# Attention with four heads at once, one in each quarter of the partitions, by tiles of queries

## The chip, the cores and the metric

The kernel runs on one core of a Trainium2 chip. The metric is device time in microseconds (us), from the first to the last work of one execution. All arithmetic is float32.

## The reference, cut to what matters

Two layers follow each other; each adds an attention branch and a feed-forward branch to its input `x` of 4 batches x 512 tokens x 512 features. The change lies in the attention of the second layer (`L1_attn`):

```python
c_kv = hidden_states @ W_DKV + b_DKV                 # 128 latent features
k = (c_kv @ W_UK + b_UK).reshape(b, s, H, D)         # H = 16 heads, D = 128
v = (c_kv @ W_UV + b_UV).reshape(b, s, H, D)
c_q = hidden_states @ W_DQ + b_DQ                    # 384 latent features
q = (c_q @ W_UQ + b_UQ).reshape(b, s, H, D)
q_r = q @ W_QR                                       # 128 -> 64
k_r = k @ W_KR
def rope(x):
    x1, x2 = (x[..., :half], x[..., half:])          # half = 32
    first = x1 * cos - x2 * sin
    return jnp.concatenate([first, jnp.zeros_like(first)], axis=-1)
q = q.at[..., :RD].set(rope(q_r))                    # RD = 64
k = k.at[..., :RD].set(rope(k_r))
scores = jnp.einsum('bqhd,bkhd->bhqk', q, k) / jnp.sqrt(jnp.float32(D))
probs = jax.nn.softmax(scores, axis=-1)
ctx = jnp.einsum('bhqk,bkhd->bqhd', probs, v).reshape(b, s, H * D)
return ctx @ W_O + b_O
```

Of the 128 features of a head, 64 are plain, 32 are rotated and 32 are zero, so a score is a sum over 96 products: three times 32.

## The kernel before, in words

The program has three stretches. From 0 to about 970 us come the first layer (a test-time-training attention and a ternary feed-forward, whose products all go through the helper at L117) and the latents of the second. From there to 1138.5 us runs the second layer's mixture of experts (pools `d_...`, products at L969, L1032 and L1062), with the preparation of the attention's first weights beside it (`fold`, biases, cosines and sines, and `lv`, the key latents with tokens on partitions). The rest, to the end at 2031.2 us, is the attention (pools `e_...`).

**Weights.** The 16 heads are four groups `hg` of four (`HPG`). `fold` prepares a group: it multiplies the rotated part into the up-projection weights (`uk`, `uq0` to `uq2`, products `pw`, L868) and W_UV into W_O (`vo`, products `pvo`, L886), so that values are never formed: a context is a product of probabilities with the key latents `lv`, and the output a product of contexts with `vo`. `fold` is a generator; one step of it is taken in a head's turn, ahead of the group that needs it.

**One head.** The attention loops over 64 units (group, batch, head).
- `queries_keys` makes kT and qT, 96 features x 512 tokens: one product for pk (L1174), three for pq (L1182). ScalarE (ACT) copies the 64 plain rows with their bias (L1175, L1186). `rotate` makes the 32 rotated rows: two operations on VectorE (DVE; L1157, L1163, each bias and cosine or sine) and a subtraction on GpSimd (POOL, L1167).
- `exponentials` makes the scores of one tile of 128 queries x 512 keys (sc, L1192), the negated row maximum on DVE (mx, L1194) and the exponential on ACT with its row sum (L1197). `scaled` is the reciprocal on DVE (L1201) and the scaling on ACT (L1202).
- `softmax` transposes each tile of probabilities in blocks of 32x32 on DVE (tt, L1221). `turn` brings the blocks to their partitions with 16 DMAs from SyncE's queue (SP; prT, L1252), each 64 KB: 32 partitions with four runs of 512 bytes.
- `context` is four products over the keys (pc, L1260) and a copy on ACT into ctxT (L1262).
- When the four heads of a (group, batch) have contexts, `outputs` multiplies ctxT with vo in four steps, by Strassen's seven products of halves with one bank `px` that is read between partial sums (p and px, L1303; 256-column products). The sums of its left operands run on POOL, and DVE adds the results into y (L1324). The last (group, batch) goes through `project_out` instead (po, L1360), with whole products.
- The first and the last head turn their probabilities by transposes on TensorE (`turned_at_once`).

**Order.** `pin` keeps the order on an engine as the program gives it. In the turn of unit i stand, one after the other: the projections of head i, scores and softmax and the turn of head i-1, one step of the outputs of a finished (group, batch), the context of head i-3, a step of `fold`. prT has three buffers; scores have four PSUM banks (ps_sc), projections, contexts, outputs and folds share three (ps_pj), and px has one.

Of the kernel before, what the change touches and what calls it, by code (L numbers as in the profile page):

```python
# [18 lines left out]
P = 128  # L19
# [36 lines left out]
def trunk_kernel(ctx: ExitStack, tc: tile.TileContext, a: dict, out: bass.AP):  # L56
# [761 lines left out]
    trig_k = lat.tile([P, L], F32, tag="trig_k", name="trig_k")  # L818
    trig_q = lat.tile([P, L], F32, tag="trig_q", name="trig_q")
    wqr = lat.tile([P, RD], F32, tag="W_QR", name="W_QR")  # L820
    wkr = lat.tile([P, RD], F32, tag="W_KR", name="W_KR")
    buk = lat.tile([P, H], F32, tag="b_UK", name="b_UK")
    buq = lat.tile([P, H], F32, tag="b_UQ", name="b_UQ")
# [11 lines left out]
    bo_part = lat.tile([P, HS], F32, tag="bo_part", name="bo_part")  # L835
    ones = lat.tile([P, P], F32, tag="ones", name="ones")
# [8 lines left out]
    def group_tiles(pool, hg):  # L845
        w = {nm: pool.tile([P, HPG, D], F32, tag=nm, name=f"{nm}_{hg}", bufs=1) for nm in ups}
        w["vo"] = pool.tile([P, HPG, HS], F32, tag="vo", name=f"vo_{hg}", bufs=1)
        return w

    def fold(w, hg, wk, psum, bufs, ahead=1, rows=nc.sync):  # L850

        heads = slice(hg * HPG, (hg + 1) * HPG)
        for nm, src in zip(ups, up_srcs):
            nc.sync.dma_start(out=w[nm][:, :, :RD], in_=src.rearrange("p (h d) -> p h d", h=H)[:, heads, :RD])
# [7 lines left out]
        for i in range(n + 1 + ahead):  # L862
            k = i - ahead - 1
            if 0 <= k < n - 1:
                wt, wr, to = turned.pop(k), wqr if k else wkr, w[ups[k]]
                pw = psum(f"pw_{hg}_{i}").rearrange("p (h d) -> p h d", h=HPG)[:, :, :RD]
                for h in range(HPG):
                    pin(nc.tensor.matmul(pw[:, h, :], lhsT=wt[:, h, :], rhs=wr, start=True, stop=True))  # L868
                pin(nc.scalar.copy(to[:, :, RD:], pw))
# [13 lines left out]
        wt = turned.pop(n - 1)  # L883
        for h in range(HPG):
# [17 lines left out]
    with ExitStack() as px:  # L902
# [197 lines left out]
        for e in range(E):  # L1100
            if e == 1:
# [7 lines left out]
                first = fold(w0, 0, wk, lambda nm: psp.tile([P, 512], F32, tag="pa", name=nm), 1)  # L1109
                nc.sync.dma_start(out=buk, in_=a["b_UK"])  # L1110
                nc.sync.dma_start(out=buq, in_=a["b_UQ"])
                for k in range(E):
                    nc.sync.dma_start(
                        out=trig_k[RD:, :].rearrange("p (k e j) -> p k e j", k=NCHUNK, e=E)[:, :, k],
                        in_=a["trig"][:, k * P : (k + 1) * P].rearrange("p (k j) -> p k j", k=NCHUNK),
                    )
# [6 lines left out]
            if e == 2:  # L1123

                for wr, bias in ((wkr, buk), (wqr, buq)):
                    pb = psp.tile([P, 512], F32, tag="pa", name="pb")
                    nc.tensor.matmul(pb[RD:, :H], lhsT=wr, rhs=bias, start=True, stop=True)
                    nc.vector.tensor_copy(bias[RD:, :], pb[RD:, :H])
                pb = psp.tile([P, 512], F32, tag="pa", name="pbuv")
                nc.tensor.transpose(pb[:, :H], buv16, ident[:H, :H])  # L1130
                nc.vector.tensor_copy(buv, pb[:, :H])
                nc.vector.tensor_scalar_mul(buq[:RD, :], buq[:RD, :], scale)
                tc.keep_in_program_order(nc.vector.tensor_scalar_mul(trig_q[RD:, :], trig_k[RD:, :], scale))
# [12 lines left out]
    with ExitStack() as px:  # L1146
# [5 lines left out]
        def rotate(t, ps, bias, trig, nm):  # L1152

            mid = RD + HALF
            t1 = wk.tile([P, L], F32, tag="t1", name=f"t1_{nm}")
            pin(
                nc.vector.scalar_tensor_tensor(  # L1157
                    t1[RD:mid, :], ps[RD:mid, :], bias[RD:mid, :], trig[RD:mid, :], ALU.add, ALU.mult
                )
            )  # L1160
            t2 = wk.tile([P, L], F32, tag="t2", name=f"t2_{nm}")
            pin(
                nc.vector.scalar_tensor_tensor(  # L1163
                    t2[RD:mid, :], ps[mid:, :], bias[mid:, :], trig[mid:, :], ALU.add, ALU.mult
                )
            )
            nc.gpsimd.tensor_sub(t[RD:mid, :], t1[RD:mid, :], t2[RD:mid, :])  # L1167

        def queries_keys(hg, b, h, w):
            nm = f"{hg}_{b}_{h}"  # L1170
            hh = hg * HPG + h
            kT = wk.tile([P, L], F32, tag="kT", name=f"kT_{nm}")
            pk = ps_pj.tile([P, L], F32, tag="pj", name=f"pk_{nm}")
            pin(nc.tensor.matmul(pk, lhsT=w["uk"][:, h, :], rhs=ckv[:, b, :], start=True, stop=True))  # L1174
            pin(nc.scalar.activation(kT[:RD, :], pk[:RD, :], AF.Identity, bias=buk[:RD, hh : hh + 1], scale=1.0))  # L1175
            rotate(kT, pk, buk[:, hh : hh + 1], trig_k, f"k{nm}")
            qT = wk.tile([P, L], F32, tag="qT", name=f"qT_{nm}")
            pq = ps_pj.tile([P, L], F32, tag="pj", name=f"pq_{nm}")
            nq = QC // P
            for i in range(nq):  # L1180
                pin(
                    nc.tensor.matmul(  # L1182
                        pq, lhsT=w[f"uq{i}"][:, h, :], rhs=cqs[hg, b][:, i, :], start=(i == 0), stop=(i == nq - 1)
                    )
                )
            pin(nc.scalar.activation(qT[:RD, :], pq[:RD, :], AF.Identity, bias=buq[:RD, hh : hh + 1], scale=scale))  # L1186
            rotate(qT, pq, buq[:, hh : hh + 1], trig_q, f"q{nm}")
            return qT, kT

        def exponentials(qT, kT, i, nm):  # L1190
            ps = ps_sc.tile([P, L], F32, tag="sc", name=f"sc_{nm}_{i}")
            pin(nc.tensor.matmul(ps, lhsT=qT[:KQ, i * P : (i + 1) * P], rhs=kT[:KQ, :], start=True, stop=True))  # L1192
            mx = wk.tile([P, 1], F32, tag="mx", name=f"mx_{nm}_{i}", bufs=4)
            pin(nc.vector.tensor_reduce(mx, ps, AX.X, ALU.max, negate=True))  # L1194
            sm = wk.tile([P, 1], F32, tag="sm", name=f"sm_{nm}_{i}", bufs=4)
            pr = wk.tile([P, L], F32, tag="pr", name=f"prob_{nm}_{i}", bufs=4)
            pin(nc.scalar.activation(pr, ps, AF.Exp, bias=mx, scale=1.0, accum_out=sm))  # L1197
            return pr, sm

        def scaled(pr, sm):  # L1200
            pin(nc.vector.reciprocal(sm, sm))  # L1201
            pin(nc.scalar.mul(pr, pr, sm))  # L1202
            return pr

        def probabilities(qT, kT, nm):

            last = None
            for i in range(E):
                now = exponentials(qT, kT, i, nm)
                if last:  # L1210
                    yield scaled(*last)
                last = now
            yield scaled(*last)

        def softmax(qT, kT, nm):

            tt = wk.tile([P, L // 32, 2, E, K], F32, tag="tt", name=f"tt_{nm}")

            def turn_blocks(i, pr):
                pin(  # L1220
                    nc.vector.transpose(  # L1221
# [310 lines left out]
```

## Time and profile before

| | |
|---|---|
| median of 3 runs | 2030.62 us (2025.25 to 2031.38) |
| the profiled execution: time and span | 2031.2 us, in one span that starts with the first and ends with the last work |
| busy share of the span | TensorE (PE) 97%, DVE 65%, ACT 42%, POOL 31% |
| attention stage, first pk at 1138.5 us to the end | 892.7 us; PE busy 882.3, DVE 646.3, ACT 478.7, POOL 277.9 |
| largest groups in that stage | scores 230.6 us busy in 512 passes, contexts 219.6 in 488 recorded, pq 175.3 in 384, pk 66.0 in 128 |

The profile counts each float32 product as two passes of the systolic array; "x8" is four products. "Busy" of a pass is from its start to its modelled end, and passes overlap, so the distance from start to start is the price of a pass. A line names the engine, the line of the kernel, the operation, "output<-inputs", the shape as partitions x elements, and how many. In the timeline a row is a run of like instructions, with its start and its length in us. A DMA is issued by an engine's queue (SPq is SyncE's): its row there is the time of the issue, and "to landing" the time from the start of the issue until the data are there.

### The profile page before, as it was taken

How to read it: one execution, taken by the hardware profiler on the slowest of the kernel's cores; microseconds unless marked ns; L12 is line 12 of the kernel's file. 1: busy time of each engine (PE TensorE's matmuls, PEld its weight loads, DVE VectorE, ACT ScalarE, POOL GpSimd, SP SyncE). 2: the span in 40 equal slices, each digit the busy share in tenths (PEclk: the TensorE clock that was granted, in tenths of full speed). 3: DMA queues.
4: the chain of work that ended last, by engine and by line, in shares of the span. 5: the costliest groups of instructions: out<-in, count | busy, mean ns of one | idle time of the engine just before them, and what ended most of it. 6: DMA issues, size and time to landing. Idle time of an engine off the chain costs nothing.

```text
span 2031.2 us, 30926 instructions
## 1 busy us (share of the span) xinstructions
PE 1970.7 (97%) x10550; PEld 1258.7 (62%) x10550; DVE 1318.6 (65%) x2760; ACT 863.1 (42%) x1763; POOL 631.4 (31%) x707
## 2 busy tenths in 40 slices
PE   8999999999999999998999999999999999999999
PEld 6777676767767676744777645555555555555555
DVE  5545657475666565664555787777777777777773
ACT  2233334334334342421322365555555555555552
POOL 4334342434243342421000232223223232354320
PEclk9999999999999999999999999999999999999999
DMA  6757566646465465645821144344434443433333
GB/s 161 208 132 210 142 181 168 182 120 180 115 168 166 127 182 150 210 136 186 290 82 57 57 106 116 94 106 112 109 94 113 106 112 81 101 98 89 93 98 94
DMA packets 318472, 270.92 MB, mean 133 GB/s; under 512 B 87659, under 2 KB 239404, under 8 KB 317676
## 3 DMA queue, kind: packets, MB, share of 16 engines
q1 hardware_dynamic: 298080, 237.31, 43.2%
q0 software_dynamic: 8736, 26.31, 4.4%
q10 hardware_dynamic: 11500, 5.32, 0.9%
q8 instruction: 85, 1.39, 0.3%
q14 instruction: 71, 0.58, 0.1%
HBM read 174.18 MB, written 34.87 MB: 103 GB/s over the span
## 4 chain that ended last, share of the span: by engine, by line
PE 48%; DVE 2%; ACT 1%; SPq 0%; issue 0%; DMA 0%; DVEq 0%; ACTq 0%
PE pc L1260 10%; PE sc L1192 10%; PE pq L1182 8%; PE px L1303 5%; PE p L1303 4%; PE epg L969 3%; PE pk L1174 3%; PE epu L969 1%; PE epo L1032 1%; PE po L1360 1%; PE eox L1062 1%; PE pw L868 1%; PE pvo L886 1%; ACT prob L1197 1%; PE eo L1062 1%; SPq L1252 0%
## 5 line engine op out<-in xcount | busy, mean ns | idle before, releaser
L1197 ACT ACTIVATE prob<-sc,mx 128x512 f32<-128x512 f32 x256 | 174.3, 683 | 164.2 <-DVE mx L1194 159.4
L1192 PE MATMUL sc<-kT,qT 96*128 96x512 f32 x512 | 230.6, 592 | 1.5 <-DVE prT_head L1241 1.3
L1260 PE MATMUL pc<-prT,lv 128*128 128x512 f32 x488 | 219.6, 592 | 0.4 <-DMA prT<-tt 0.4
L1221 DVE STREAM_TRANSPOSE tt<-prob 128x512 f32<-128x512 f32 x248 | 170.3, 706 | 55.1 <-ACT prob L1202 45.7
L1167 POOL TENSOR_TENSOR kT<-t_k,t_k 32x512 f32<-32x512 f32 x64 | 80.6, 1259 | 380.3 <-PE pq L1182 235.6
L117 PE MATMUL pf<-xT,wg 128*128 128x256 f32 x704 | 174.1, 389 | 5.7 <-DMA wg<-in_wg 3.6
L1182 PE MATMUL pq<-cq,uq 128*128 128x512 f32 x384 | 175.3, 592 | 1.7 <-ACT ctxT L1262 1.7
L1202 ACT ACTIVATE prob<-prob,sm 128x512 f32<-128x512 f32 x256 | 176.5, 713 | 0.0
L1192 PEld LDWEIGHTS sc<-kT,qT 96*128 96x128 f32 x512 | 96.8, 190 | 124.1 <-issue 118.2
L117 PE MATMUL pf<-xT,wu 128*128 128x256 f32 x704 | 169.6, 384 | 3.3 <-DMA wu<-in_wu 3.3
L1194 DVE TENSOR_REDUCE mx<-sc 128x1 f32<-128x512 f32 x256 | 168.0, 677 | 2.3 <-PE sc L1192 0.3
L117 PE MATMUL pd<-wd,hid 128*128 128x512 f32 x352 | 165.7, 600 | 0.9 <-DMA wd<-in_wd 0.7
L117 PEld LDWEIGHTS pf<-xT,wg 128*128 128x128 f32 x704 | 132.7, 193 | 32.4 <-issue 9.3
L1260 PEld LDWEIGHTS pc<-prT,lv 128*128 128x128 f32 x488 | 92.5, 190 | 92.9 <-issue 88.8
L117 PEld LDWEIGHTS pf<-xT,wu 128*128 128x128 f32 x704 | 135.1, 193 | 23.4 <-DMA wu<-in_wu 4.7
L478 DVE SCALAR_TENSOR_TENSOR hid<-pf,us,sg 128x256 f32<-128x256 f32 x88 | 41.8, 477 | 159.5 <-ACT sg L477 159.1
L1182 PEld LDWEIGHTS pq<-cq,uq 128*128 128x128 f32 x384 | 72.8, 190 | 93.9 <-issue 81.8
L314 POOL TENSOR_SCALAR sk<-k,m 128x256 f32<-128x256 f32 x64 | 60.6, 957 | 180.1 <-PE pz L117 167.9
L421 POOL TENSOR_SCALAR gh<-grad,m 128x256 f32<-128x256 f32 x64 | 61.6, 972 | 152.0 <-DVE grad L390 130.2
L117 PEld LDWEIGHTS pd<-wd,hid 128*128 128x128 f32 x352 | 63.5, 190 | 59.4 <-issue 44.0
L477 ACT ACTIVATE sg<-pf,gs 128x256 f32<-128x256 f32 x88 | 41.4, 473 | 135.9 <-PE pf L117 135.5
L1167 POOL TENSOR_TENSOR qT<-t_q,t_q 32x512 f32<-32x512 f32 x64 | 80.6, 1260 | 56.3 <-DVE t_q L1163 56.3
(326 smaller groups left out, 3579.0 us busy)
## 6 DMA issues: line engine op xcount, KB each, us to landing
prT<-tt SPq DMA_DIRECT2D x992, 64.0 KB, 2.0
wd<-in_wd SPq DMA_DIRECT2D x176, 256.0 KB, 3.1
wg<-in_wg SPq DMA_DIRECT2D x88, 256.0 KB, 3.0
wu<-in_wu SPq DMA_DIRECT2D x88, 256.0 KB, 3.2
cq<-lat_d SPq DMA_DIRECT2D x48, 256.0 KB, 3.9
rows<-rows SPq DMA_DIRECT2D x128, 66.0 KB, 2.2
kv<-rows POOLq DMA_DIRECT2D x32, 264.0 KB, 4.3
gu<-in_gu SPq DMA_DIRECT2D x3, 2048.0 KB, 8.6
```

What stands on the lines that cost most here:

```text
L117: nc.tensor.matmul(out, lhsT=lhsT, rhs=rhs, start=start, stop=stop, skip_group_check=True)
L421: nc.gpsimd.tensor_scalar_mul(gh[:, :, h, :], g, m2[:, h : h + 1])
L969: nc.tensor.matmul(ps, lhsT=w[:, c, :], rhs=x[:, c], start=start and c == 0, stop=c == 1, skip_group_check=True)
L1167: nc.gpsimd.tensor_sub(t[RD:mid, :], t1[RD:mid, :], t2[RD:mid, :])
L1182: nc.tensor.matmul(pq, lhsT=w[f"uq{i}"][:, h, :], rhs=cqs[hg, b][:, i, :], start=(i == 0), stop=(i == nq - 1))
L1192: pin(nc.tensor.matmul(ps, lhsT=qT[:KQ, i * P : (i + 1) * P], rhs=kT[:KQ, :], start=True, stop=True))
L1194: pin(nc.vector.tensor_reduce(mx, ps, AX.X, ALU.max, negate=True))
L1197: pin(nc.scalar.activation(pr, ps, AF.Exp, bias=mx, scale=1.0, accum_out=sm))
L1202: pin(nc.scalar.mul(pr, pr, sm))
L1221: nc.vector.transpose(out=tt[:, :, :, i, :], in_=pr.rearrange("p (kb e j) -> p kb e j", e=2, j=K))
L1260: pin(nc.tensor.matmul(pc, lhsT=lv[:, b, k, :], rhs=prT[:, k, :], start=(k == 0), stop=(k == E - 1)))
L1303: nc.tensor.matmul(ps[:, q, :], lhsT=a[:, k, q * P : (q + 1) * P], rhs=w[:, k, :], start=start and k == 0 and q == 0, stop=k == 1, skip_gr ...
```

## The change

The unit becomes one (group, batch) with four heads at once, and a block of work one tile of 128 queries for these four heads. The three pieces of 32 features (even plain, odd plain, rotated) lie in tiles of their own; in each, head h has the partitions 32h to 32h+31. There are again 64 blocks: 16 units of four query tiles.

- `fold` writes the weights in two halves, plain and rotated (cosine part of all four heads, sine part of all four), with the score's scale multiplied in; the tile for vo is allocated later.
- `up_projected` makes 128 columns (32 of each of four heads) for keys and for queries: one and three products again. Pieces 0 and 1 are a bias copy on ACT over 128 partitions. Pieces 2 and 3 are one DVE operation each over 128 partitions, and the subtraction on POOL runs over 128 partitions. One of the four is made in each block, for the next unit, in the order 2, 3, 0, 1.
- `scores` issues 12 products of 32 rows for a block, round the four row quarters, each head into a bank of its own.
- `softmax` interleaves the four heads' steps; `prT` has two buffers, and each of the 16 DMAs now moves one 2 KB run from each of 32 partitions.
- The context of block n-1 stands behind the scores, the projections, the output step and the fold step of block n.
- The outputs of the last unit take the same Strassen steps, with one more bank and the left sums on DVE; finished quarters are stored as they come. The transposes on TensorE for the first and last head and `project_out` are gone.
- In the mixture stage, cosine and sine are copied to all four quarters by six more DMAs on SP, and the biases come from 32 small products, each into a quarter of the columns.

The diff, without the removed functions, which are shown above:

```diff
-    trig_k = lat.tile([P, L], F32, tag="trig_k", name="trig_k")
-    trig_q = lat.tile([P, L], F32, tag="trig_q", name="trig_q")
+    cos, sin = (lat.tile([P, L], F32, tag=nm, name=nm) for nm in ("cos", "sin"))
-    buk = lat.tile([P, H], F32, tag="b_UK", name="b_UK")
-    buq = lat.tile([P, H], F32, tag="b_UQ", name="b_UQ")
+    b_up = lat.tile([P, 2, E, NHG], F32, tag="b_up", name="b_up")
...
     def group_tiles(pool, hg):
+        return {nm: pool.tile([P, 2, HPG * RD], F32, tag=nm, name=f"{nm}_{hg}", bufs=1) for nm in ups}
...
-                pin(nc.scalar.copy(to[:, :, RD:], pw))
+                pin(
+                    nc.scalar.mul(
+                        to[:, 1].rearrange("p (x h r) -> p h x r", x=2, h=HPG),
+                        pw.rearrange("p h (x r) -> p h x r", x=2),
+                        scale if k else 1.0,
+                    )
+                )
...
+                for t, rows in ((cos, slice(0, HALF)), (sin, slice(HALF, RD))):
+                    for k in range(E):
+                        nc.sync.dma_start(
+                            out=t[:HALF].rearrange("p (k e j) -> p k e j", k=NCHUNK, e=E)[:, :, k],
+                            in_=a["trig"][rows, k * P : (k + 1) * P].rearrange("p (k j) -> p k j", k=NCHUNK),
+                        )
+                    for r in quarters[1:]:
+                        nc.sync.dma_start(out=t[r], in_=t[:HALF])
                 nc.sync.dma_start(out=ckv, in_=lat_d[0].rearrange("p b k x -> p b (k x)"))
...
+                for j, wr in enumerate((wkr, wqr)):
+                    by_head = b_raw[:, j].rearrange("p (hg h) -> p h hg", h=HPG)
+                    for m in range(E):
+                        t = ident[:, m:RD:2] if m < 2 else wr[:, HALF * (m - 2) : HALF * (m - 1)]
+                        for h, r in enumerate(quarters):
+                            nc.tensor.matmul(
+                                pb[r, j, m],
...
+        def up_projected(u, m, to):
+            hg, b = u
+            def columns(w):
+                return w[:, 0, m::2] if m < 2 else w[:, 1, (m - 2) * P : (m - 1) * P]
+            nq = QC // P
+            for j, nm in enumerate("kq"):
+                ps = ps_pj.tile([P, L], F32, tag="pj", name=f"p{nm}_{hg}_{b}_{m}")
+                srcs = [(f"uq{i}", cqs[u][:, i, :]) for i in range(nq)] if j else [("uk", ckv[:, b, :])]
+                for i, (w, x) in enumerate(srcs):
+                    pin(
+                        nc.tensor.matmul(
+                            ps, lhsT=columns(ws[hg][w]), rhs=x, start=(i == 0), stop=(i == len(srcs) - 1)
+                        )
+                    )
+                bias = b_up[:, j, m, hg : hg + 1]
+                if m == 2:
+                    t1 = to[f"t1{nm}"] = wk.tile([P, L], F32, tag="t1", name=f"t1{nm}_{hg}_{b}")
+                    pin(nc.vector.scalar_tensor_tensor(t1, ps, bias, cos, ALU.add, ALU.mult))
+                elif m == 3:
+                    t = to[f"{nm}2"] = wk.tile([P, L], F32, tag=f"{nm}r", name=f"{nm}r_{hg}_{b}")
+                    pin(nc.vector.scalar_tensor_tensor(t, ps, bias, sin, ALU.add, ALU.mult))
+                    nc.gpsimd.tensor_sub(t, to.pop(f"t1{nm}"), t)
+                else:
+                    t = to[f"{nm}{m}"] = wk.tile([P, L], F32, tag=f"{nm}{m}", name=f"{nm}{m}_{hg}_{b}", bufs=2 - m)
+                    pin(nc.scalar.activation(t, ps, AF.Identity, bias=bias, scale=scale if j else 1.0))
+                yield
+        def scores(qk, i, nm):
+            ps = [ps_sc.tile([P, L], F32, tag="sc", name=f"sc_{nm}_{i}_{h}") for h in range(HPG)]
+            for n, c in enumerate((0, 2, 1)):
+                for h, r in enumerate(quarters):
+                    pin(
+                        nc.tensor.matmul(
+                            ps[h],
+                            lhsT=qk[f"q{c}"][r, i * P : (i + 1) * P],
+                            rhs=qk[f"k{c}"][r, :],
+                            start=(n == 0),
+                            stop=(n == 2),
+                        )
+                    )
+            return ps
+        def softmax(ps, nm, to):
+            tt = wk.tile([P, 4, HPG, E, 32], F32, tag="tt", name=f"tt_{nm}")
+            prs = {}
+            for h in range(HPG + 2):
+                if h < HPG:
+                    mx = wk.tile([P, 1], F32, tag="mx", name=f"mx_{nm}_{h}", bufs=4)
+                    pin(nc.vector.tensor_reduce(mx, ps[h], AX.X, ALU.max, negate=True))
+                    sm = wk.tile([P, 1], F32, tag="sm", name=f"sm_{nm}_{h}", bufs=4)
+                    pr = wk.tile([P, L], F32, tag="pr", name=f"prob_{nm}_{h}", bufs=4)
+                    pin(nc.scalar.activation(pr, ps[h], AF.Exp, bias=mx, scale=1.0, accum_out=sm))
+                    prs[h] = pr, sm
+                if 0 <= h - 1 < HPG:
+                    pr, sm = prs[h - 1]
+                    pin(nc.vector.reciprocal(sm, sm))
+                    pin(nc.scalar.mul(pr, pr, sm))
+                if h >= 2:
+                    pr, sm = prs.pop(h - 2)
+                    pin(
+                        nc.vector.transpose(
+                            out=tt[:, :, h - 2], in_=pr.rearrange("p (k kq j) -> p kq k j", kq=4, j=32)
+                        )
+                    )
+                if h < HPG + 1:
+                    yield
+            prT = to[nm] = wk.tile([P, 4, HPG, E, 32], F32, tag="prT", name=f"prT_{nm}")
+            for qb in range(4):
+                for kq in range(4):
+                    nc.sync.dma_start(out=prT[32 * kq : 32 * kq + 32, qb], in_=tt[32 * qb : 32 * qb + 32, kq])
+            yield
+        def context(prT, b, ctxT, i, nm):
+            pc = ps_pj.tile([P, L], F32, tag="pj", name=f"pc_{nm}")
+            at = prT.rearrange("p qb h k j -> p (qb h) k j")
+            for k in range(E):
+                pin(nc.tensor.matmul(pc, lhsT=lv[:, b, k, :], rhs=at[:, :, k, :], start=(k == 0), stop=(k == E - 1)))
+            pin(
+                nc.scalar.copy(
+                    ctxT.rearrange("p eh h el (i c j) -> p i c (eh h el) j", c=2, j=K)[:, i],
+                    pc.rearrange("p (c x j) -> p c x j", c=2, j=K),
+                )
+            )
...
-        def left_operands(c):
+        def left_operands(c, eng):
...
+            final = (hg, b) == (NHG - 1, B - 1)
...
+            def store(qh, oh):
+                if hg == NHG - 1:
+                    for e in (2 * qh, 2 * qh + 1):
+                        cols = slice(oh * half, (oh + 1) * half)
+                        nc.sync.dma_start(out=rows_of(out, b)[:, e, cols], in_=y[b][:, e, cols])
...
+            o = left_operands(c, nc.vector if final else nc.gpsimd)
...
+            if final:
+                p4 = bank(ps_sc, "sc", "p4")
+                block_product(p4, o["a22"], r["t4"])
+                add(p4, 1, 0)
             block_product(x, o["s2"], r["t2"], False)
             add(p2, 0, 0)
+            store(0, 0)
             add(x, 0, 1)
...
+        units = [(hg, b) for hg in range(NHG) for b in range(B)]
+        nu = len(units)
+        order = (2, 3, 0, 1)
+        ws, cs, qk, probs = {0: w0}, {}, {}, {}
+        folds, outs = iter(()), iter(())
+        def advance(n, steps):
+            for _ in range(n):
+                next(steps, None)
+        def context_of(n):
+            u, i = divmod(n, E)
+            hg, b = units[u]
+            if i == 0:
+                cs[u] = wk.tile([P, 2, HPG, 2, P], F32, tag="ctxT", name=f"ctxT_{u}")
+            context(probs.pop(f"{u}_{i}"), b, cs[u], i, f"{u}_{i}")
+        cqs[units[1]] = batch_latents(*units[1])
+        qk[0] = {}
+        for m in order:
+            for _ in up_projected(units[0], m, qk[0]):
+                pass
+        for u, (hg, b) in enumerate(units):
+            if b == 0 and hg + 1 < NHG:
+                pool = (lat, wk)[(hg + 1) % 2]
+                ws[hg + 1] = group_tiles(pool, hg + 1)
+                folds = fold(
+                    ws[hg + 1],
+                    pool,
+                    hg + 1,
+                    wk,
+                    lambda nm: ps_pj.tile([P, 512], F32, tag="pj", name=nm),
+                    2,
+                    2,
+                    nc.gpsimd,
+                )
+            if u + 2 < nu:
+                cqs[units[u + 2]] = batch_latents(*units[u + 2])
+            qk[u + 1] = {}
+            for i in range(E):
+                n = E * u + i
+                soft = softmax(scores(qk[u], i, f"{u}"), f"{u}_{i}", probs)
+                ups_next = up_projected(units[u + 1], order[i], qk[u + 1]) if u + 1 < nu else iter(())
+                advance(2, soft)
+                advance(1, ups_next)
+                advance(1, soft)
+                advance(1, ups_next)
+                advance(1, soft)
+                if u > 0 and i == 1:
+                    outs = outputs(*units[u - 1], ws[units[u - 1][0]], cs.pop(u - 1))
+                advance(1, outs)
+                advance(1, soft)
+                advance(1, folds)
+                if n > 0:
+                    context_of(n - 1)
+                advance(1, soft)
+                if hg == NHG - 1:
+                    nc.gpsimd.tensor_add(y[b][:, i, :], y[b][:, i, :], bo)
+            qk.pop(u)
+        advance(1, outs)
+        context_of(E * nu - 1)
+        for _ in outputs(*units[-1], ws[NHG - 1], cs.pop(nu - 1)):
+            pass
```

## The prediction

> **What bounds the kernel now.** I read the page first: span, engines, and the chain that ended last.
>
> ```profile
> span 2031.2 us, 30926 instructions
> ...
> PE 1970.7 (97%) x10550; PEld 1258.7 (62%) x10550; DVE 1318.6 (65%) x2760; ACT 863.1 (42%) x1763; POOL 631.4 (31%) x707
> ...
> PE pc L1260 10%; PE sc L1192 10%; PE pq L1182 8%; PE px L1303 5%; PE p L1303 4%; PE epg L969 3%; PE pk L1174 3%; PE epu L969 1%; PE epo L1032 1%; PE po L1360 1%; PE eox L1062 1%; PE pw L868 1%; PE pvo L886 1%; ACT prob L1197 1%; PE eo L1062 1%; SPq L1252 0%
> ```
>
> The chain is TensorE. The attention stage runs from the first pk at 1138.5 to the end, 892.7 us, and the windows put TensorE busy there in 98% or more, DVE near 74%, ACT near 55%. So TensorE work that goes is gained as long as nothing else becomes late. The timeline gives the prices:
>
> ```profile
> 1986.61 1.89 PE L1303 MATMUL p<-vo,ctxT 128*128 128x256 f32 x8
> ...
> 1987.88 10.25 SPq L1252 DMA_DIRECT2D prT<-tt  x16
> ...
> 1988.34 1.89 PE L1303 MATMUL px<-t_ops,s_ops 128*128 128x256 f32 x8
> ...
> 1990.06 3.60 PE L1192 MATMUL sc<-kT,qT 96*128 96x512 f32 x8
> ...
> 1993.50 1.89 PE L1303 MATMUL p<-t_ops,s_ops 128*128 128x256 f32 x8
> ```
>
> A float32 product is two passes. From the start of one row to the start of the next, a 512-column pass takes 3.44/8 = 0.43 us and a 256-column pass 1.73/8 = 0.216 us, whether 96 or 128 rows are used. Beside it stands the row this prediction turns on: SP needs 10.25 us to issue the 16 DMAs that turn one head's probabilities, 0.64 us each. A head takes 892.7/64 = 13.9 us, and a head's probabilities have two heads' time before they are read, so today that costs nothing.
>
> For small products side by side the trace has the column-tiled ones of the first stage:
>
> ```profile
> 415.84 0.59 PE L117 MATMUL pz<-gsum,bones 128*128 128x256 f32 x2
> 416.37 1.08 PE L117 MATMUL pz<-wq_bd,sk 128*32 128x128 f32 x32
> 417.27 0.63 PE L117 MATMUL pso<-wq_bd,wh 128*32 128x64 f32 x32
> 417.83 1.09 PE L144 MATMUL pj<-ident,xt 128*128 128x128 f32 x8
> 418.76 0.59 PE L117 MATMUL pd<-wd,hid 128*128 128x512 f32 x1
> ```
>
> 32 passes of 128 columns start within 0.90 us, 28 ns each; the full-width transposes of the same length take 0.93/8 = 116 ns. Four column tiles run at once, in float32, issued round the four tiles as the new scores will be. Going in and out costs: two 256-column passes want 0.43 us and take 0.53, so 0.1; out about the same, 0.1 to 0.2.
>
> **The change, part by part.** A block is one tile of 128 queries for four heads; 64 blocks replace 64 heads.
>
> Scores. Before: 512 passes x 0.43 = 220 us. After: per block 12 products, 24 passes, four at a time, so 6 x 0.43 = 2.58, plus two switches of 0.15 = 2.88; x 64 = 184. Gain 36. Row tiles are not in the trace; bounds: four at once (column row, 2.58) to none at once (24 x 0.43 = 10.3). I take the column row: same machine, same float32, same issuing order.
>
> The rule that speaks against it is in the Trainium skill, "TensorE: Matmul & The Clock Gate", Part 3, "Measured speedup vs the span model": four row tiles gave 3.07 times there, not 4. By the page a set would take 0.56 us, 50 us more TensorE work. The column row says 116/28, about 4, and I sum by it.
>
> A dearer set has a row of its own: pso, the same column tiles with 64 columns. Its 32 passes take 0.56 us (417.27 to 417.83), 17.5 ns each, where half of a 128-column pass at the 256-column rate is 0.216/4 = 0.054: 3.1 times. I hold this for the short pass (the new ones have 512 columns), and keep it as the upper bound: sets of 0.43 x 4/3.1 = 0.56, so 64 x 6 x 0.13 = 50 us more.
>
> Projections and contexts keep their counts, 512 passes each: 220 + 220. Outputs: before 15 units x 56 x 0.216, 32 passes of 0.43 and 32 transposes of 0.11 = 199; after 16 x 56 x 0.216 = 194. Folds 23 in both. Without waits the stage is 184 + 220 + 220 + 194 + 23 = 841, plus about 7 of head and tail (the first block waits on its rotation, the last context copy, the last add and store: 3.9 us lie behind the last matmul now) = 848, against 892.7: 45 us less.
>
> Off the path: the 256 rotations of 32x512 on DVE (0.75 us each) become 64 of 128x512, 128 subtractions on POOL (1.26) become 32, 128 bias copies on ACT become 64. DVE and ACT are not the bound, so I cost this at nothing.
>
> Earlier stages: 32 tiny column-tiled products for the biases (32 passes of 128x4 take 0.8 us in the trace), 1.5 us on TensorE. The cosine and sine copies hold SP some 9 us instead of 3 and are ahead of ckv, wanted only 25 us later: nothing.
>
> The probabilities' turn is where a wait is added. Before, the context of head i-3 stands after the scores of head i-1: two heads' slack, three prT buffers. After, the context of block n-1 stands on TensorE behind the scores, projections and output step of block n: one block's slack. Behind a waiting context on TensorE queue the next scores, so a late turn stops everything. Follow it from the end of block n-1's scores. The order of the built program puts the output step's adds on DVE ahead of the last two transposes. So: switch 0.15, projections 3.44, output step 3.46, result 0.2 = 7.25; add 0.69, reciprocal 0.16, scale on ACT 0.71, last transpose 0.71 = 9.5. Then 16 issues on SP, and the last lands 1.43 us after its issue ends (median of the 992 prT DMAs now: 2.0 from start, 0.6 of it issue). Each new DMA moves one 2 KB run from each of 32 partitions instead of four of 512 B. Its issue is not in the trace. The nearest rows, back to back:
>
> ```profile
> 775.84 1.29 SPq L625 DMA_DIRECT2D xl<-xe_d  x3
> ...
> 30.63 5.61 SPq L294 DMA_DIRECT2D rows<-rows  x12
> ...
> 227.57 1.88 SPq L127 DMA_DIRECT2D xt<-in_x  x3
> ...
> prT<-tt SPq DMA_DIRECT2D x992, 64.0 KB, 2.0
> ```
>
> xl (128 partitions, one 2 KB run each) 0.43; rows (16 partitions) 0.47; xt (64 partitions, one 2 KB run each) 0.63; prT (32 partitions, four runs) 0.64. Number of runs and bytes don't order these: 128 runs cost 0.43 and 0.64. The count of partitions does: 128 and 16 cheap, 64 and 32 dear. Bounds 0.43 to 0.64; I take 0.64, because the new DMA has the partitions of the one and the single run of the other dear row.
>
> So the turn is there 9.5 + 10.3 + 1.43 = 21.2 us after the scores. Context 3.44, then the next scores 0.15 + 2.58: 27.4 us for two blocks, 54.8 for a unit of four. TensorE's own work is 2.88 + 3.44 + 3.46 + 3.44 = 13.2 a block, 11.5 where a unit's output begins, 51.2 a unit. Wait: 3.6 x 14 middle units = 51. The first unit has no outputs (last transpose at 8.2): 26.2 against 19.6 for two blocks, 12 us. The last has no projections (7.9): 12 us, and 6 for the last block's turn. Folds put 23 us of products into the waiting, but also a transpose of 0.7 on DVE ahead of the chain: I take 5 off. 51 + 12 + 12 + 6 - 5 = 76.
>
> Sum: -45 + 76 + 1.5 = +32 on the profiled 2031.2. That execution lies 0.6 above the median 2030.6, so 2062.
>
> The Trainium skill would leave the wait out: "DMA: Bandwidth & Descriptors", "Issuing engines are not separate DMA queues", calls the time to initiate a DMA usually small beside the DMA. Here it is 0.64 beside 2.0, and 16 stand in a row. By the page the stage would be 848 and the kernel 1987; the row decides.
>
> **Rivals.** *The issue gets cheap, faster.* If one run per partition costs 0.47 (rows), the turn is there at 9.5 + 7.5 + 1.43 = 18.4, and two blocks need 24.6, under the 25.6 of TensorE's work: no wait in the middle units. First unit 8, last 7, end 4.5: 20 in all. -45 + 20 + 1.5 = -24: 2007. For it: fewer descriptors, as few as rows' or fewer. Against: xt has one run per partition and costs 0.63. It decides at about 0.575 us an issue, where waits are worth 45.
>
> *Row products run two at a time, much slower.* Sets of 0.86: 165 us more TensorE work, waits shrink to about 26: -45 + 165 + 26 + 1.5, 2180. All one after another, near 2490. For it: the two passes of one product share a row tile, and four banks are written at once, which no row shows. Against: the column tiles have the same two passes.
>
> *Between*: an issue of 0.55 to 0.6, or a chain about 1 us shorter than I add up: 2025 to 2037.
>
> **How the numbers follow.** Forecast case (0.64, four at once) 0.58, its own range 2040 to 2092: down 22 if the chain is 0.75 us shorter than I add up (two chains in a unit, so 1.5 x 15 units); up 30 for sets of 0.56 by the pso row, 50 us of work of which some 20 only fill waits. Cheap issue 0.22 (2000 to 2024). Between 0.09. Rows in twos or worse 0.11. A range of 2003 to 2092 leaves out the last case and the ends of the first two. About 0.3%, 6 us, is what a measurement of this kernel can tell from no change. Faster 0.24 (cheap issue and a little), same 0.09, slower 0.67.
>
> **What would show it.** Right: prT issues at 0.64 us on SP; TensorE idle put down to DMA prT in front of the contexts, 60 to 80 us in all, most in the first and last unit per block; score sets of four starting within tens of ns, 0.43 us a set; DVE's share falling. Wrong: issues near 0.45 and no such idle time; score passes at over 0.11 us each on average; TensorE waiting for DVE or ACT instead.

## The result, and the profile after

The changed kernel takes 2091.28 us (median of 4 runs, 2087.96 to 2101.61), beside 2028.95 us for the kernel before in the same rounds: ratio 1.031, 95% interval 1.028 to 1.035. The forecast was 2062, a loss of 31 us; the measured loss of 62 us is twice that, and the time lies at the upper end of the range.

The page of the profile after: span, engines, chain.

```profile
span 2090.7 us, 32374 instructions
...
PE 1966.6 (94%) x11626; PEld 1235.9 (59%) x11626; DVE 1175.8 (56%) x2579; ACT 816.7 (39%) x1695; POOL 512.0 (24%) x611
...
PE pc L1251 8%; SPq L1243 8%; PE sc L1205 6%; PE pq L1182 6%; PE px L1298 3%; PE p L1298 3%; PE epg L973 3%; PE pk L1182 2%; DMA prT<-tt 2%; PE epo L1036 1%; PE epu L973 1%; DVE tt L1234 1%; ACT prob L1230 1%; DVE y L1320 1%; PE eox L1066 1%
```

The chain is no longer TensorE alone: SP's issues (L1243) are 8% of it and the landings of prT 2%. TensorE fell from 97% to 94% busy, and its busy time by only 4 us, though the new scores need far less of it. The waits in front of TensorE, from the first projection of the attention stage on (engine, line, what it waited for: us, times, longest):

```profile
PE pc L1251 <- DMA prT<-tt: 48.6, 20, 6.0
PE pc L1251 <- issue: 4.8, 6, 2.1
PE pc L1251 <- DVE tt L1234: 2.7, 4, 1.1
PE pc L1251 <- DVE sm L1229: 2.5, 2, 1.3
```

All four stand before pc, the context, where waits were forecast; the whole view lists 65.9 us, of which 3.6 stand before other products. It names ACT, DVE or "issue" for some, but a context reads only prT and lv, and in each of the 35 pauses before a context that are longer than 0.15 us the last landing of a prT lies 0.1 to 1.3 us ahead of its start: they are waits for the turn. A block in the timeline, with the prices of its scores:

```profile
1600.99 36.27 SPq L1243 DMA_DIRECT2D prT<-tt  x48
...
1602.93 1.14 PE L1205 MATMUL sc<-k,q 32*128 32x512 f32 x8
...
1603.89 1.04 PE L1205 MATMUL sc<-kr,qr 32*128 32x512 f32 x8
...
1604.75 1.04 PE L1205 MATMUL sc<-k,q 32*128 32x512 f32 x8
...
1605.72 1.12 PE L1182 MATMUL pk<-ckv,uk 128*128 128x512 f32 x2
```

The row products run four at a time: eight passes (four products) every 0.86 us, and a block's scores take 1605.72 - 1602.93 = 2.79 us. SP issues the turns of three blocks in 36 us; at 0.633 us an issue (the median from start to start) it is busy with them for 30 of these, with pauses of 4.2 and 1.8 us between the blocks.

What the forecast did not have is in the windows of the trace (us, busy us of each engine, then the granted clock of TensorE and the DMA share). They follow a grid of 3.41 us, on which the granted clock changes:

```profile
core 0: us, PE busy (x) PEld busy (x) DVE busy (x) ACT busy (x) POOL busy (x), PEclk, DMA share, GB/s
1396.79:1400.20 3.41, 3.23 (x12) 1.90 (x10) 3.38 (x8) 2.54 (x6) 3.13 (x3) 1.00 0.39 96
1400.20:1403.61 3.41, 1.23 (x3) 0.68 (x4) 2.16 (x5) 1.55 (x4) 0.23 (x1) 1.00 0.25 63
1403.61:1407.02 3.41, 3.41 (x5) 1.35 (x4) 0.00 (x0) 0.00 (x0) 0.00 (x0) 0.50 0.40 96
1407.02:1410.44 3.42, 3.42 (x26) 1.13 (x24) 0.00 (x0) 0.58 (x1) 0.00 (x0) 1.00 0.45 111
```

The context in the third and fourth of these rows, with the idle time ahead of it in brackets:

```profile
1402.38 5.37 PE L1251 MATMUL pc<-prT,lv 128*128 128x512 f32 x8 [2.37 <-DMA prT<-tt]
```

The wait leaves TensorE 1.23 of 3.41 us busy, and in the next window the clock is 0.50: the context's passes, 0.429 us apart otherwise, start 0.853 us apart, and the context takes 5.37 us instead of the 3.67 of one that starts after a wait at full clock (in the run with filled waits, below). The attention stage has 15 windows at half clock (one behind the last products is left out, here and in every count); before the change it had none. Each costs at most half of 3.41 us, less where TensorE is idle in part of it.

To compare kernels I split the stage by the starts of TensorE's passes: work is every pass at its full-clock distance, waits are longer distances ahead of another product, half clock is 1.71 us for each window, an upper bound. (The rest, about 10 us, is the first pass of a group and what lies behind the last pass. The stage after is counted from 1139.08 us, 1.3 us behind the start of its first pk. The terms are estimates: they move by some us with what is taken for a pause.)

| profiled, us | stage | work | waits | half-clock windows |
|---|---|---|---|---|
| before | 892.7 | 876.7 | 5.7 | 0 |
| after | 951.6 | 843.6 | 72.9 | 15 = 25.6 |
| difference | +58.9 | -33.1 | +67.2 | +25.6 |

### The profile page after: what moved, and what is told of

It reads as the page before. It is cut to its first block, busy times and chain, and to the rows that moved or that the text cites. A ratio compares the mean times of both kernels' runs of the same rounds, so it can differ in the third digit from the quotient of the medians.

```text
span 2090.7 us, 32374 instructions
## 1 busy us (share of the span) xinstructions
PE 1966.6 (94%) x11626; PEld 1235.9 (59%) x11626; DVE 1175.8 (56%) x2579; ACT 816.7 (39%) x1695; POOL 512.0 (24%) x611
## 4 chain that ended last, share of the span: by engine, by line
PE 36%; SPq 8%; DVE 3%; DMA 3%; ACT 2%; issue 2%; DVEq 0%; ACTq 0%
PE pc L1251 8%; SPq L1243 8%; PE sc L1205 6%; PE pq L1182 6%; PE px L1298 3%; PE p L1298 3%; PE epg L973 3%; PE pk L1182 2%; DMA prT<-tt 2%; PE epo L1036 1%; PE epu L973 1%; DVE tt L1234 1%; ACT prob L1230 1%; DVE y L1320 1%; PE eox L1066 1%
## 5 line engine op out<-in xcount | busy, mean ns | idle before, releaser
L1251 PE MATMUL pc<-prT,lv 128*128 128x512 f32 x512 | 255.8, 646 | 62.8 <-DMA prT<-tt 48.6
L1251 PEld LDWEIGHTS pc<-prT,lv 128*128 128x128 f32 x512 | 101.3, 206 | 186.3 <-issue 169.7
L1230 ACT ACTIVATE prob<-prob,sm 128x512 f32<-128x512 f32 x256 | 182.9, 720 | 60.4 <-DVE sm L1229 60.4
L1234 DVE STREAM_TRANSPOSE tt<-prob 128x512 f32<-128x512 f32 x256 | 178.7, 701 | 37.9 <-ACT prob L1230 30.9
L1205 PE MATMUL sc<-k,q 32*128 32x512 f32 x1024 | 143.7, 616 | 1.3 <-ACT prob L1225 1.3
L1253 ACT COPY ctxT<-pc 128x512 f32<-128x512 f32 x64 | 37.4, 585 | 218.4 <-PE pc L1251 218.4
L1288 POOL TENSOR_TENSOR s_ops<-ctxT 128x512 f32<-128x512 f32 x15 | 18.9, 1261 | 341.8 <-ACT ctxT L1253 341.8
L1205 PEld LDWEIGHTS sc<-k,q 32*128 32x128 f32 x1024 | 47.8, 185 | 80.9 <-issue 75.7
```

The source lines that it names most:

```text
L1205: nc.tensor.matmul(ps[h], lhsT=qk[f"q{c}"][r, i * P : (i + 1) * P], rhs=qk[f"k{c}"][r, :], start=(n == 0), stop=(n == 2),)
L1234: nc.vector.transpose(out=tt[:, :, h - 2], in_=pr.rearrange("p (k kq j) -> p kq k j", kq=4, j=32))
L1251: pin(nc.tensor.matmul(pc, lhsT=lv[:, b, k, :], rhs=at[:, :, k, :], start=(k == 0), stop=(k == E - 1)))
```

## The experiments

Theory A: a turn issued as 16 DMAs, one after the other on SP, is late for a context that has one block of slack; and each wait that empties most of a 3.41 us window halves the clock in the next. Rivals were that the row products pull the clock down, and that the chain on DVE and ACT decides and not SP. Each ratio below is to the kernel before in the same rounds, with its 95% interval; work, waits and half-clock windows are counted as in the table.

**Half the issues.** 8 DMAs of 64 partitions.

```diff
-                for kq in range(4):
-                    nc.sync.dma_start(out=prT[32 * kq : 32 * kq + 32, qb], in_=tt[32 * qb : 32 * qb + 32, kq])
+                for kq in range(2):
+                    nc.sync.dma_start(out=prT[64 * kq : 64 * kq + 64, qb], in_=tt[64 * kq : 64 * kq + 64, qb])
```

> Edit: the turn of a block is 8 DMAs of 64 partitions instead of 16 of 32; the same bytes, but the blocks of probabilities land in the wrong places (the output is not the reference's). Theory A (TensorE waits for a late turn, because SP issues 16 DMAs of 0.63 us one after the other; and each long wait then costs more, because the clock is halved in the 3.41 us window that follows one with little work): 5 us less before each context, waits fall from 73 to about 6 us, half-clock windows from 15 to 1 or 2; 2000 us (1995 to 2010). Rival B (the 32-row products pull the clock down, whatever the waits): the 15 half-clock windows stay, 2024. Rival C (the chain on DVE and ACT and the one block of slack decide, not SP): 2075 to 2090.

Measured: 2009.4 us (ratio 0.989, 0.986 to 0.991), waits 13.7, 3 half-clock windows, work 839.9. DVE, ACT and the row products are unchanged, so C falls, and B as the cause of the 15 windows: the issues make the waits, and all but three windows go with them. The time is 9 us above the point of A: 3.8 us are one wait of a context in the last unit that the trace puts down to a store of the output, which also goes through SP. The issues of one turn, and that wait:

```profile
1966.33 4.95 SPq L1243 DMA_DIRECT2D prT<-tt  x8
```

```profile
PE pc L1251 <- DMA out<-y: 3.8, 1, 3.8
```

**Fill the waits.** The same kernel as after, with work that nobody reads.

```diff
             pc = ps_pj.tile([P, L], F32, tag="pj", name=f"pc_{nm}")
+            for _ in range(fill):
+                pin(nc.tensor.matmul(pc, lhsT=lv[:, b, 0, :], rhs=ckv[:, b, :], start=True, stop=True))
...
+            fill = {0: 6, 2: 6, 4: 3, E * nu - 1: 6}.get(n, 2 if n % E == 0 or n >= E * (nu - 1) - 1 else 0)
```

> Edit: products that nobody reads are put ahead of the contexts that wait longest (first unit 6, 6 and 3 products, the first context of every unit and all of the last unit 2 each, the last context 6), 51 products or 44 us of TensorE work in all, into the bank that the context then overwrites. Theory A (the half clock comes from the idle wait itself): the filled waits leave 1 or 2 half-clock windows of 15, so 22 us less, and the fill is longer than the wait in some blocks, 2 to 4 us: 2071 (2066 to 2078), faster though TensorE does more. Rival B (row products pull the clock): no window fewer, 2092 to 2096.

Measured: 2085.73 us (ratio 1.0265, 1.0242 to 1.0288). The time lies outside both expectations, between them. The windows tell more: 2 at half clock instead of 15. One block, with the fill (L1250) where the earlier wait was:

```profile
1396.43 1.88 PE L1250 MATMUL pc<-ckv,lv 128*128 128x512 f32 x4
1398.97 3.67 PE L1253 MATMUL pc<-prT,lv 128*128 128x512 f32 x8 [0.66 <-DMA prT<-tt]
```

The context behind it takes 3.67 us, not 5.37. The fill was 47.4 us (55 products, not the 51 I had counted) and 38.2 us of waits stayed: 85.6 together where 72.9 had been, so 12.7 went into blocks whose wait was shorter than the fill, where I had allowed 2 to 4. -22 + 13 = -9, close to the 8 us between the two profiles. With the row products unchanged, the 14 windows that stood at filled contexts go: there the half clock comes from the idle time. Of the two windows in this run, one (1885.39) is new, at a context without fill that waits 2.02 us; the other (1161.77) was there before, behind the row products of the second block (last section).

**Two blocks of slack.**

```diff
-                if u > 0 and i == 1:
+                if u > 0 and i == 2:
...
-                if n > 0:
-                    context_of(n - 1)
+                if n > 1:
+                    context_of(n - 2)
...
+        advance(1, outs)
+        context_of(E * nu - 2)
```

> Edit: the context of block n-2 instead of n-1 stands behind block n, and the outputs of a unit begin one block later; still two buffers for the turned probabilities. Theory A: all waits between the second block and the last ones go (a turn of 23.5 us has 27 or more), 4 to 5 us stay at the first context, 6 at the last, SP sets the pace in the first and last unit by a little; waits 13 to 16, three or four half-clock windows (6 us): 2009 (2003 to 2016). Rival B (row products pull the clock): some 20 more, 2025 to 2030. Rival D (two buffers are too few, SP then waits for the context two blocks back and the turn is late again): waits of 1 us or more a block stay, 2050 and up.

Measured: 2013.59 us (ratio 0.991, 0.988 to 0.994). Work 843.0, waits 9.8, 3 half-clock windows. TensorE in a block of the middle, then the largest group of its waits in the stage:

```profile
1563.98 1.89 PE L1298 MATMUL p<-t_ops,s_ops 128*128 128x256 f32 x8
1565.71 1.89 PE L1298 MATMUL px<-t_ops,ctxT 128*128 128x256 f32 x8
1567.44 3.60 PE L1251 MATMUL pc<-prT,lv 128*128 128x512 f32 x8
```

```profile
PE pc L1251 <- DMA prT<-tt: 5.7, 3, 3.1
```

The context starts 1.73 us after the last output product began, which is that product's length: no wait. What is late next is SP, and nobody minds: it now waits for a buffer that the context two blocks back releases (second line), which rival D named, but in blocks 30 to 35 there are 21 to 25 us from this release to the context that needs the turn, and the turn has landed 11.4 to 12.3 us after the release.

```profile
SPq L1243 <- DVE tt L1234: 63.1, 40, 10.4
SPq L1243 <- PE pc L1251: 53.9, 47, 2.1
```

**Two queues.**

```diff
-                    nc.sync.dma_start(out=prT[32 * kq : 32 * kq + 32, qb], in_=tt[32 * qb : 32 * qb + 32, kq])
+                    eng = nc.gpsimd if kq % 2 else nc.sync
+                    eng.dma_start(out=prT[32 * kq : 32 * kq + 32, qb], in_=tt[32 * qb : 32 * qb + 32, kq])
```

> Edit: 8 of the 16 DMAs of a turn are issued by SP, the other 8 by POOL; everything else as after the change. Theory A: POOL's issues take 0.55 to 0.66 us in this trace, so both queues are through in about 5 us, the turn is 4 to 5 us earlier and waits fall from 73 to 6 to 12 us: 2004 (1998 to 2014). Rival C (DVE and ACT chain and slack decide): 2075 to 2090. Rival E (POOL's DMAs land later or hold up POOL's subtractions and sums so that scores or outputs wait): 2020 to 2060.

Measured: 2016.48 us (ratio 0.993, 0.990 to 0.995), just outside what A allowed; waits 15.4, 3 half-clock windows. POOL issues one in 0.50 us, but both queues' DMAs now take longer to land, 2.8 and 2.7 us instead of 2.0 (how much of the waits that left was not measured apart):

```profile
prT<-tt SPq DMA_DIRECT2D x512, 64.0 KB, 2.8
prT<-tt POOLq DMA_DIRECT2D x512, 64.0 KB, 2.7
```

**Two blocks of slack, two queues at the ends.** POOL issues half of the turns of the first two and last three blocks (`ends`).

```diff
-                    nc.sync.dma_start(out=prT[32 * kq : 32 * kq + 32, qb], in_=tt[32 * qb : 32 * qb + 32, kq])
+                    eng = nc.gpsimd if kq % 2 and ends else nc.sync
+                    eng.dma_start(out=prT[32 * kq : 32 * kq + 32, qb], in_=tt[32 * qb : 32 * qb + 32, kq])
...
-                soft = softmax(scores(qk[u], i, f"{u}"), f"{u}_{i}", probs)
+                soft = softmax(scores(qk[u], i, f"{u}"), f"{u}_{i}", probs, n < 2 or n >= E * nu - 3)
```

> Edit: on top of the version with two blocks of slack, POOL issues half of the turns of the first two and the last three blocks. Theory A: the waits left there are 4 to 5 us at the last contexts with two half-clock windows behind them (3.4 us); they go, the middle stays as it is: 6 to 7 us less than that version in the same round of work, so 2006 (2000 to 2012). Rival E (POOL's issues land later, as the 2.7 us to landing in the run with two queues hints): no more than 2 us less.

Measured: 2000.97 us (6 runs; ratio 0.986, 0.982 to 0.989). Work 845.3, waits 4.2, 2 half-clock windows, both at the second block, behind row products (last section). No wait for a turn is left. Its profile is 5.7 us below that of the version with slack alone, as expected; the two were not run in the same rounds, and their intervals overlap a little. It is the fastest version that computes the reference, 1.4% below the kernel before.

**The kernel before with one head of slack.** 96-row scores, heads one by one.

```diff
-            if i >= 3:
-                hg, b, h = units[i - 3]
-                context(probs.pop(i - 3), b, cs[hg, b], h, f"{i - 3}")
+            if i >= 2:
+                hg, b, h = units[i - 2]
+                context(probs.pop(i - 2), b, cs[hg, b], h, f"{i - 2}")
...
-        context(probs.pop(nu - 2), b, at[1], HPG - 2, "next", ps_sc, "sc")
```

> Edit on the kernel before, with its 96-row scores: the context of head i-2 instead of i-3, so one head of slack instead of two. Theory A (the slack against a turn of 16 issues of 0.63 us decides, not the row products): in the trace of before a head's last turn lands 21.3 us after its scores begin, and the context would stand 20.65 behind them in the middle and 13.8 in the first heads: waits of 0.6 us a head in the middle (about 30 us), 7 in each of the first three or four (25), some at the end (5), and four or five half-clock windows (8): 2095 (2070 to 2110). Rival B (the waits belong to the four-heads-at-once form): 2031 to 2045.

Measured: 2103.83 us (ratio 1.036, 1.033 to 1.039). Work 879.8, waits 68.1, 6 half-clock windows. The largest group of waits:

```profile
PE pc L1260 <- DMA prT<-tt: 30.9, 12, 7.5
```

Taking one head of slack from the old kernel makes it at least as slow as the new one, without a row product in it. The loss belongs to the slack.

**Row products quarter by quarter.**

```diff
-            for n, c in enumerate((0, 2, 1)):
-                for h, r in enumerate(quarters):
+            for h, r in enumerate(quarters):
+                for n, c in enumerate((0, 2, 1)):
```

> Edit on the kernel after: the 12 row products of a block go head by head (three products in one quarter, then the next), not round the quarters. Theory A (four run at once because neighbours are in different quarters): 24 passes of 0.43 us are 10.3 us instead of 2.6 a block, no waits for the turn are left: 2091 - 73 - 26 + 64 x 7.7 = about 2485; half the clock on top if single-quarter products count as little work (up to 3100). Rival F (the order does not matter, the array fills itself from its queue): 2085 to 2095.

Measured: 2201.82 us (one run). Both expectations were wrong. A block's scores take 5.67 us, against 2.79 round the quarters and the 10.3 of strict order:

```profile
1599.41 0.69 PE L1205 MATMUL sc<-k,q 32*128 32x512 f32 x1
1599.83 0.59 PE L1205 MATMUL sc<-kr,qr 32*128 32x512 f32 x1
1599.94 0.91 PE L1205 MATMUL sc<-k,q 32*128 32x512 f32 x2
1600.37 0.59 PE L1205 MATMUL sc<-kr,qr 32*128 32x512 f32 x1
```

Starts 0.11 us apart show products of two heads running beside each other, then a pause: about two at a time. The order is worth 2.9 us a block, 184 us in all, and with scores this long the waits shrink to 24.6.

**A quarter of the issues.** 4 DMAs of 128 partitions.

```diff
-                for kq in range(4):
-                    nc.sync.dma_start(out=prT[32 * kq : 32 * kq + 32, qb], in_=tt[32 * qb : 32 * qb + 32, kq])
+                nc.sync.dma_start(out=prT[:, qb], in_=tt[:, qb])
```

> Edit on the kernel after: the turn of a block is 4 DMAs of 128 partitions instead of 16 of 32; same bytes, wrong places (the output is not the reference's). Theory A with the price going by the number of partitions: 0.43 to 0.47 us an issue, 1.8 us a turn instead of 10.1; no waits for a turn outside the last context, 2 half-clock windows: 2003 (1998 to 2010), 2 to 8 below the run with 8 DMAs. Rival G (an issue's price goes by the bytes or the number of runs, four times as many here): 1.5 us and more an issue, 2010 or more.

Measured: 2002.27 us (ratio 0.985, 0.982 to 0.987), waits 6.6, one half-clock window. The time is A's, but not by its price:

```profile
1609.57 2.41 SPq L1242 DMA_DIRECT2D prT<-tt  x4
```

Four issues of 128 partitions and 256 KB take 2.41 us, 0.60 each and 0.64 from start to start: as much each as one of 32 partitions and 64 KB. Among these DMAs the price goes neither by partitions nor by bytes.

## Why the prediction was wrong, by its steps

**Scores, projections, outputs: right.** Sets of four passes at 0.43 us; scores 220 to 183.4 (forecast 184) by the starts of the passes, 63 blocks at 2.79 us and the second block 7.82, where banks came late; work 843.6 against 841 in the forecast. The rivals with slower row products fell. The Trainium skill ("TensorE: Matmul & The Clock Gate", Part 3, "Measured speedup vs the span model") has 3.07 times for four row tiles; here four products take the 0.86 us of one, and with the switches a block reaches 24 x 0.43 / 2.79 = 3.7.

**The turn's chain: right.** SP's issues stand 0.633 us apart (forecast 0.64), the last transposes behind the output adds, and TensorE waits before the contexts: 72.9 us, forecast 76, with the longest in the first unit (5.8 and 6.3) and before the last context (5.9). The rule that gave 0.64 was wrong, though: I let the number of partitions order the prices, and 128 partitions cost the same. That the price came out right was luck as far as the rule goes: prT before and after are both moves from SBUF to SBUF, the cheap xl row is not; whether that orders the price stays open.

**The sum: here it failed.** "-45 + 76 + 1.5 = +32" charges a wait its own length and every product behind it the full clock. 848 + 76 = 924 was the forecast for the stage, 951.6 the result; up to 25.6 of the 27.6 between them are the 15 half-clock windows, a term that the sum put at nothing without a reason. The filled waits and the kernel with two blocks of slack showed that they go with the waits, all but one or two at the second block. I had read the clock only in the page's row of tenths, 9 throughout, and in one mean of the stage. The trace of before had the price, in the windows of its first stage (same columns as above):

```profile
51.89:55.30 3.41, 1.11 (x6) 1.03 (x7) 3.08 (x11) 1.40 (x2) 3.03 (x7) 1.00 0.23 37
55.30:58.72 3.42, 3.42 (x10) 2.68 (x9) 1.97 (x5) 0.00 (x0) 1.59 (x2) 0.50 0.55 173
```

The forecast's own terms held part of it: its 30 us of waits in the first and last unit are long ones, and ten of the 15 windows lie there. Its 3.6 us in a middle unit are two waits of about 1.8 us, which by the border in the last section would have halved little; in fact the middle waits were uneven, up to 3.0 us, and five windows followed.

The upper end of my range, 2092, held the time by luck, for a reason that did not happen (row sets of 0.56 us).

**Rivals.** "The issue gets cheap" fell at 0.633; the runs with 8 and 4 DMAs show what it would have brought: 2009 and 2002, beside its 2007.

## What to carry to other kernels

In these traces a wait of TensorE costs its length and then, if it empties most of a window of the clock, up to 1.7 us more: look at the granted clock window by window around the waits that the kernel already has, and put that price into the sum for each wait that a change adds. When a buffer is turned by many small DMAs from one queue, count issues x distance and compare it with the time between the producer and the consumer on the engine that sets the pace; one more block of slack turned a loss of 3% into a gain of 1%, without touching a single product.

## What the runs showed of the hardware

- The granted clock of TensorE changed only on a grid of 3.41 us and only between 1.00 and 0.50. The Trainium skill ("TensorE: Matmul & The Clock Gate", Part 1, "What's actually happening") says so: a free-running window of 4096 cycles, 3413 ns, and half rate after an idle one. But its advice ("Why this matters for your kernels") to avoid gaps of over about 3 us is not strict enough here: idle times of 2.29 us (before 1968.88) and 2.37 us (before 1402.38) were followed by half clock, while one of 2.65 us that fell across two windows was not:

```profile
1622.07:1625.48 3.41, 2.64 (x11) 1.61 (x9) 3.38 (x8) 2.55 (x7) 2.76 (x3) 1.00 0.40 96
1625.48:1628.89 3.41, 1.53 (x4) 0.84 (x5) 1.58 (x4) 0.97 (x2) 0.00 (x0) 1.00 0.24 58
1628.89:1632.31 3.42, 3.42 (x17) 1.32 (x20) 0.00 (x0) 0.58 (x1) 0.00 (x0) 1.00 0.42 102
```

  By the windows' busy times the border is near 1.5 us of 3.41, and not sharp: after 1.23, 1.33 (before 1970.22) and 1.49 (before 2052.14) the clock was halved, after 1.53 not, and neither after 1.48 (third row below). In other runs the clock was halved after as much as 1.63 (kernel with half the issues, before 715.11).
- Row products that come few at a time seem to count for less. In the second block they came in ones and twos, because banks were late, and 2.44 us busy were still followed by half clock:

```profile
1157.85:1161.26 3.41, 2.44 (x7) 0.59 (x6) 3.41 (x8) 2.67 (x7) 0.00 (x0) 1.00 0.00 0
1161.26:1164.67 3.41, 3.11 (x16) 1.56 (x17) 1.60 (x4) 1.47 (x4) 0.00 (x0) 0.50 0.00 0
1168.08:1171.50 3.42, 1.48 (x4) 0.38 (x2) 2.87 (x7) 1.91 (x4) 2.12 (x2) 1.00 0.40 99
1171.50:1174.91 3.41, 0.00 (x0) 0.00 (x0) 1.61 (x4) 1.48 (x4) 0.19 (x1) 1.00 0.39 96
```

  The same is seen in that block in all seven kernels that issue the row products round the quarters (2.14 to 2.44 us busy each time), while the kernel before was not halved there after 2.13 us. In two of them, half the issues and two queues at the ends, the clock stayed at half after a window of 3.41 us busy with hardly anything but row products. If each of these passes is put at a quarter of its 0.43 us, an estimate, the windows that these products lead into at full clock had 0.6 to 1.5 us. So the rival that row products pull the clock may hold for one or two windows of each of these kernels. No run changed this alone, and as a cause it is not shown.
- An issue of prT cost SP 0.63 to 0.65 us from start to start with 32, 64 and 128 partitions; POOL needed 0.50 for one of 32, but when both queues shared the turns, a DMA landed 2.7 to 2.8 us after its issue began instead of 2.0.
- Row products in an order that leaves neighbours in the same quarter still overlapped, about two at a time: 24 passes in 5.67 us, 0.236 us each, where one alone takes 0.43 (one run).
